# Layer 3's first chunk multiplied inside the last attention head

## The chip, the cores and the metric

The kernel runs on one core of a Trainium2 chip. Its time is the device time of one launch in microseconds (us). Before the change the median of three runs is 1751.03 us (1750.17 to 1754.02). TensorE (PE) does matrix products, VectorE (DVE), ScalarE (ACT) and GpSimd (POOL) do elementwise work, and SyncE (SP) issues most DMAs. PEld is TensorE's weight loading.

## The reference

Four graph layers follow each other on a graph of 2708 nodes with 512 features; each takes the layer-normed, relu'd features and adds its result to them. What matters here is the end of layer 2, attention with 8 heads, and the start of layer 3:

```python
# layer 2, per head h
e = where(adj > 0, leaky_relu(f1[:, None] + f2[None, :], 0.2), -9e15)
out = elu(softmax(e) @ Wh)
x = x + concat_heads(out)
# layer 3
h = maximum(layernorm(x), 0)
agg = (adj > 0) @ h / deg
x = x + relu(concat(h @ W_self + b_self, agg @ W_nb + b_nb) @ W_comb + b_comb)
```

The kernel has the weights of layer 3 multiplied together beforehand, so that layer 3 is one product of h with each of two fused matrices (`wfs` for the node itself, `wfn` for the neighbours), one bias row (`b3`), and an aggregation over the adjacency of the neighbour product.

## The kernel before

**Chunks.** The 2708 rows are cut into 22 chunks of 128 rows (`NC`; the last has 20). The functions with a chunk number `c` below handle one such chunk.

**Attention.** Ten units run one after the other: heads 0 and 7 in two halves of the target columns each, heads 1 to 6 whole. A unit has 22 steps, one per source chunk, so there are 220 steps; unit 9, the second half of head 7, has steps 198 to 219. In a step `s` the loop at L1443 to L1467 first prepares step `s + 3`: `scale` (ACT, tile `whs`, L1051 and L1053) and `make` (DVE, the attention weights, tile `t`, L1067). Then `multiply` (PE, L1297) adds step `s` into PSUM tiles `av` and `sums`. There are four buffers of `t` (`TILES`). After its last step a unit's sums are copied out by ACT (`evict`, L1337) and stored on SP's queue to `avT` and `sumT` (L1339).

**Order of the work.** The instructions are traced in program order, and a planner then orders those of each engine by its own costs, in favour of what stands first in the program. [...] A table `plan`, filled by `behind(step, function, chunk)`, says behind which step of the attention loop a piece of other work is written. The entries for layer 3 are counted back from the end of the attention: `(9, turn3, 0)` means step 220 - 9 = 211.

**From attention to layer 3, for one chunk.** `load3` (SP: `aT` from `avT` L1237, `sT` from `sumT` L1240, and the residual rows `x`); `turn3` (PE: a small product and four transpositions, L1246 and L1250; DVE: `rs` L1252 to L1255 and `y` L1257); `elu3` (POOL: `z = min(y, 0)` L1264; DVE: `x += max(y, 0)` L1265; ACT: Tanh and Exp of `z`, L1267 and L1268; DVE: L1269 and L1270, which use Exp(z) - 1 = (Exp(z) + 1) Tanh(z/2)); `save3` (a store of `x` on ACT's queue); `normalize3` (DVE L219, L221, ACT Sqrt L223, DVE L224, L234, tile `hn`); `transpose3` (PE L245, ACT L247, tile `hT`); `nb3` (PE: eight matmuls with `wfn`, L187; `halves` splits the result in two on ACT L298 and DVE L299); `self3` (PE: eight matmuls with `wfs`, L187; DVE adds `b3`, L1495; the store to `s3` is on ACT's queue). After these comes the aggregation (L424).

**Where they stand.** `nb3` and `self3` and the pool for their results (`ring3`) exist only after the attention: the loop over all 22 chunks at L1510 runs `nb3(c)`, `transpose3(c+1)`, `turn3(c+3)`, `normalize3(c+2)`, `save3(c+2)`, `elu3(c+3)`, `load3(c+5)`, `self3(c)`. Ahead of it, the attention's last steps do `turn3` of chunks 0 to 2, and `elu3`, `normalize3` and `transpose3` of chunk 0. `elu3`'s Tanh has a tile `th3` of its own with one buffer. Tiles tagged `t` (three buffers) hold `hn`, the `y` of `self3` and the copies of `evict`.

Of the kernel before, what the change touches and what calls it, by code (L numbers as in the profile page):

```python
# [44 lines left out]
def fast_layers(  # L45
# [46 lines left out]
    def rows(c):  # L92
        return min(R, N - c * R)

    def move(engine, dst, src):

        if dst.shape[0] == last_rows:
            cut = last_rows // 16 * 16
            engine.dma_start(dst[:cut], src[:cut])
            return engine.dma_start(dst[cut:], src[cut:])  # L100
        return engine.dma_start(dst, src)
# [106 lines left out]
    def any_product(c, po, lhsT, w, n):  # L208
        if c == NC - 1:
            product_of_last(po, lhsT, w)  # L210
        else:
            product(po, lhsT, w, n)
# [1008 lines left out]
    tails_w = tails.tile([P, len(middle), O + S], F32, name="tails_w")  # L1221
    nc.gpsimd.memset(tails_w, 0.0)
    tails_f = tails.tile([P, 3], F32, name="tails_f")
    kept3, l3_weights = {}, []


    def load3(c):
# [32 lines left out]
    def elu3(c):  # L1260

        xc, y = kept3[c]
        z = e3.tile([R, D], F32, name="z3")
        nc.gpsimd.tensor_scalar(z, y, 0.0, None, op0=ALU.min)  # L1264
        nc.vector.scalar_tensor_tensor(xc[:R], y, 0.0, xc[:R], op0=ALU.max, op1=ALU.add)  # L1265
        th = e3.tile([R, D], F32, name="th3", bufs=1)
        nc.scalar.activation(th, z, AF.Tanh, scale=0.5)  # L1267
        nc.scalar.activation(z, z, AF.Exp)  # L1268
        nc.vector.scalar_tensor_tensor(z, z, 1.0, th, op0=ALU.add, op1=ALU.mult)  # L1269
        nc.vector.tensor_tensor(xc[:R], xc[:R], z, ALU.add)  # L1270
        kept3[c] = xc

    def save3(c):
        n = rows(c)
        move(nc.scalar, x3[c * R : c * R + n, :], kept3[c][0][:n])

    def normalize3(c):
        kept3[c] = kept3[c], norm(kept3[c], R)
# [147 lines left out]
        behind(first + 2, count_neighbors, i)  # L1426

    for at_step, fn, c in (
        (16, load3, 0),
        (15, load3, 1),  # L1430
        (9, turn3, 0),
        (8, load3, 2),
        (8, elu3, 0),
        (6, normalize3, 0),
        (6, save3, 0),
        (6, turn3, 1),
        (5, load3, 3),
        (2, transpose3, 0),
        (2, turn3, 2),
        (1, load3, 4),  # L1440
    ):
        behind(len(steps) - at_step, fn, c)

    for s in range(len(steps)):
        if s == (len(units) - 3) * NC + 1:
            tails_ctx.close()
            e3_ctx = ctx.enter_context(ExitStack())
            e3 = e3_ctx.enter_context(
                tc.tile_pool(name="e3", bufs=2, side="right", reuse_waits="tile")
            )  # L1450
        if s + 6 < len(steps) and (s + 6) % NC % GROUP == 0:
            load_wh(s + 6)
        if s + 3 < len(steps):
            scale(s + 3)
            make(s + 3)
        if s + 1 < len(steps):
            compare(s + 1)
        multiply(s)
        multiply_sides(s - 1)
        for fn, args in plan.pop(s, ()):  # L1460
            if fn in (load_l3_weights, spread_nodes, split):
                with tc.issue_after(made[s]):
                    fn(*args)
            elif fn is mask:
                with tc.issue_after(scaled[s + 2]), tc.issue_after(made[s]):
                    fn(*args)
            else:  # L1467
                fn(*args)
# [4 lines left out]
    with ExitStack() as stack:  # L1473
        margin = stack.enter_context(tc.tile_pool(name="margin", bufs=1))
        margin.tile([P, 112], F32, name="margin")
        ring = stack.enter_context(tc.tile_pool(name="ring3", bufs=NC - 1, reuse_waits="tile"))
        b3 = ring.tile([P, D], F32, name="b3", bufs=1)
        nc.sync.dma_start(
            b3, bass.AP(tensor=bias3.tensor, offset=bias3.offset, ap=[[0, P], [1, D]])
        )  # L1480
        h3 = {}
        wself, wnb = l3_weights

        def nb3(c):
            pn = ps.tile([P, D], F32, name="nb3_ps", tag="ps")
            any_product(c, pn, kept3[c][1], wnb, R)
            h3[c] = halves(ring, pn, c)

        def self3(c):
            n = rows(c)  # L1490
            po = ps.tile([P, D], F32, name="self_ps", tag="ps")
            any_product(c, po, kept3.pop(c)[1], wself, R)
            y = common.tile([P, D], F32, name="y", tag="t", bufs=3)
            for own in corners if c == NC - 1 else [(slice(0, n), slice(0, D))]:
                ins = nc.vector.tensor_tensor(y[own], po[own], b3[own], ALU.add)  # L1495
                move(nc.scalar, s3[c * R : c * R + n, own[1]], y[own])
            return ins.ins

        def do(fn, c):
            if c < NC:  # L1500
                fn(c)


        elu3(1)
        normalize3(1)
        save3(1)
        elu3(2)
        for c in range(NC):
            nb3(c)
            if c:  # L1510
                do(transpose3, c + 1)
            do(turn3, c + 3)
            do(normalize3, c + 2)
            do(save3, c + 2)
            do(elu3, c + 3)
            do(load3, c + 5)
            final = self3(c)
            if c == 0:
                transpose3(1)

        e3_ctx.close()
        wk = stack.enter_context(
            tc.tile_pool(name="l3", bufs=2, side="right", reuse_waits="tile")
        )

        def weight3(m, cs):
            kt = wk.tile([R, WG], F32R, name="kt3", bufs=3)
            nc.vector.tensor_copy(by_chunk(kt, cs), pattern(m, cs))  # L1528
            return kt

        def judge():


            bad = const.tile([P, 7], F32, name="bad")

            nc.gpsimd.memset(squares[TAIL:, NC - 1], 0.0)
            nc.vector.tensor_reduce(
                bad[:, 0:1], squares.rearrange("p c g -> p (c g)"), AX.X, ALU.add
            )
            nc.vector.tensor_reduce(bad[:, 1:2], deg, AX.X, ALU.add)  # L1540
            nc.vector.tensor_tensor(bad[:, 0:1], bad[:, 0:1], bad[:, 1:2], ALU.subtract)
            nc.vector.tensor_reduce(bad[:, 2:3], deg, AX.X, ALU.min)
            nc.vector.tensor_scalar(bad[:, 2:3], bad[:, 2:3], 0.5, None, op0=ALU.is_lt)
            for i, (op, over, sign) in enumerate(((ALU.max, ALU.is_gt, 1), (ALU.min, ALU.is_lt, -1))):
                f = bad[:, 3 + i : 4 + i]
                nc.vector.tensor_reduce(f, f12.rearrange("p c h -> p (c h)"), AX.X, op)
                nc.vector.tensor_scalar(f, f, sign * F_MAX, None, op0=over)
                nc.vector.tensor_scalar(
                    bad[:, 5 + i : 6 + i], wmax[:, i : i + 1], sign * W_MAX, None, op0=over
                )  # L1550
            nc.vector.tensor_reduce(bad[:, 1:2], bad[:, 2:], AX.X, ALU.max)
            pv = ps.tile([P, 2], F32, name="verdict_ps", tag="ps")
            nc.tensor.matmul(pv[:1], ones, bad[:, 0:2], start=True, stop=True)

            differ = small.tile([1, 2], F32, name="differ")
            nc.vector.tensor_scalar(
                differ[:, 0:1], pv[:1, 0:1], float(N - P * NC), None, op0=ALU.not_equal
            )
            nc.vector.tensor_copy(differ[:, 1:2], pv[:1, 1:2])
            nc.vector.tensor_tensor(verdict, differ[:, 0:1], differ[:, 1:2], ALU.add)  # L1560

        def before3(c):
            if c == 2 * KMAX:
                with tc.issue_after(final):
                    judge()
            return load_x(x3, c), load_x(s3, c, name="sc", pool=wk, bufs=4)

        def after3(c, acc, loaded):
            n = rows(c)
            xc, sc = loaded  # L1570
            nc.vector.scalar_tensor_tensor(
                sc[:n], acc[:n], rdeg[:n, c : c + 1], sc[:n], op0=ALU.mult, op1=ALU.add
            )
            nc.vector.scalar_tensor_tensor(
                xc[:n], sc[:n], 0.0, xc[:n], op0=ALU.max, op1=ALU.add
            )
            half = max(1, n // 32) * 16 if c == NC - 1 else n
            nc.scalar.dma_start(out[c * R : c * R + half, :], xc[:half])
            if half < n:
                nc.sync.dma_start(out[c * R + half : c * R + n, :], xc[half:n])  # L1580

        aggregate(weight3, h3, before3, after3)
# [628 lines left out]
```

## Time and profile before

| | us |
|---|---|
| median of three runs | 1751.03 |
| the profiled execution, its own time | 1754.19 |
| its span, first to last instruction | 1752.3 |
| TensorE busy | 1724.1 (98%) |
| VectorE busy | 1312.2 (75%) |
| ScalarE busy | 845.6 (48%) |
| unit 9 begins on TensorE | 1309.95 |
| `nb3(0)` begins | 1354.90 |
| `nb3(1)` begins | 1368.13 |
| `nb3(2)` begins | 1376.15 |

All positions are us from the start of the span. In a timeline a row has start, length, engine, line, operation, `out<-in`, the engine's shape, and in square brackets how long the engine had been idle and what ended that. A matmul that waits in the pipeline still counts as busy, so PE's 98% is not 98% of its peak. The granted clock is TensorE's, 1.00 being full.

### The profile page before, as it was taken

The page shows a single profiled execution, that of the slowest core. Times are in us where ns is not written, and L with a number is a line of the kernel's source. Part 1 is how long each engine was busy: PE and PEld are TensorE (multiplying, and loading weights), DVE is VectorE, ACT ScalarE, POOL GpSimd, SP SyncE. Part 2 cuts the span into 40 slices and gives each one's busy share as a digit, 9 for nine tenths or more (in the row PEclk, how much of TensorE's full clock was granted, in tenths as well). Part 3 has the DMA queues.
Part 4 walks back from the last instruction along what each step waited for, and adds up shares of the span by engine and source line. Part 5 has one row for each costly group of instructions (what it writes and reads, how often), then busy time and mean ns, then how long its engine had stood idle before and what let it go on. Part 6 is the DMA issues. An engine that isn't in the chain of part 4 may idle for free.

```text
span 1752.3 us, 29486 instructions
## 1 busy us (share of the span) xinstructions
PE 1724.1 (98%) x11280; PEld 1078.8 (62%) x11280; DVE 1312.2 (75%) x1902; ACT 845.6 (48%) x1554; POOL 248.3 (14%) x252
## 2 busy tenths in 40 slices
PE   8999999999999999999999999999999999999998
PEld 5567777744468887644675665434434455588886
DVE  7759889855455556888899999999998677633334
ACT  5447777622210000366878888888794566400000
POOL 1003323311111112255000000000001222100000
PEclk9999999999999999999999999999999999999999
DMA  8436666444551111332420221022022444313221
GB/s 291 139 117 199 205 206 186 133 120 123 121 135 49 48 49 56 122 122 93 133 63 13 61 64 58 15 64 62 13 74 72 130 141 130 109 36 109 73 72 41
DMA packets 167227, 177.37 MB, mean 101 GB/s; under 512 B 84127, under 2 KB 106591, under 8 KB 166060
## 3 DMA queue, kind: packets, MB, share of 16 engines
q1 hardware_dynamic: 144428, 131.99, 27.2%
q10 hardware_dynamic: 18808, 33.37, 5.1%
q0 software_dynamic: 3840, 10.03, 1.5%
q8 instruction: 90, 1.47, 0.4%
q14 instruction: 61, 0.50, 0.1%
HBM read 111.64 MB, written 55.36 MB: 95 GB/s over the span
## 4 chain that ended last, share of the span: by engine, by line
PE 86%; DVE 8%; ACT 2%; issue 2%; DMA 1%; SPq 1%; POOL 0%; ACTq 0%; DVEq 0%; POOLq 0%
PE acc L424 36%; PE av L1297 17%; PE nb_ps L187 8%; DVE t L1067 5%; PE sums L1297 4%; PE h_ps L187 4%; PE line_ps L187 4%; PE self_ps L187 4%; PE hT_ps L245 2%; PE fused_ps L370 2%; PE wh_ps L187 1%; DVE wh_a L1114 1%; PE av_ps L1250 1%; ACT b L1085 1%; DVE f L1131 1%
## 5 line engine op out<-in xcount | busy, mean ns | idle before, releaser
L1067 DVE SCALAR_TENSOR_TENSOR t<-rb,ec,vT 128x2708 f32<-128x2708 f32 (+2 forms) x214 | 510.4, 2450 | 8.3 <-PE sums L1297 6.2
L1297 PE MATMUL av<-t,whs 128*32 128x451 f32 (+5 forms) x4432 | 445.5, 514 | 6.2 <-DVE t L1067 3.9
L424 PE MATMUL acc<-halves,kt 128*128 128x512 f32 x1848 | 426.5, 391 | 2.4 <-DVE kt L870 2.1
L424 PEld LDWEIGHTS acc<-halves,kt 128*128 128x128 f32 x1848 | 345.2, 188 | 79.7 <-DVE kt L870 6.6
L1085 ACT ACTIVATE b<-t,eb 128x2708 bf16<-128x2708 f32 (+1 forms) x119 | 285.0, 2395 | 33.3 <-DVE t L1067 33.2
L1297 PEld LDWEIGHTS av<-t,whs 128*32 128x32 f32 (+1 forms) x4432 | 193.2, 110 | 167.9 <-issue 118.5
L424 PE MATMUL acc<-halves,ar 128*128 128x512 f32 x924 | 243.6, 414 | 0.0
L424 PEld LDWEIGHTS acc<-halves,ar 128*128 128x128 f32 x924 | 172.6, 188 | 58.2 <-issue 20.6
L223 ACT ACTIVATE ln_rs<-ln_mv,eps 128x1 f32<-128x1 f32 x88 | 25.7, 295 | 306.3 <-DVE ln_mv L221 298.4
L870 DVE SCALAR_TENSOR_TENSOR kt<-lastr,index,vT 128x512 fp32r<-128x512 int16 (+3 forms) x154 | 112.5, 742 | 75.8 <-PE acc L424 75.4
L1528 DVE CAST kt<-vT 128x512 fp32r<-128x512 uint8 (+3 forms) x154 | 56.5, 368 | 131.3 <-PE acc L424 131.2
L1264 POOL TENSOR_SCALAR z<-y 128x512 f32<-128x512 f32 x22 | 44.1, 2005 | 639.5 <-DMA aT<-avT 513.6
L555 DVE TENSOR_TENSOR_SCAN cum<-ai,deg 128x512 int16<-128x512 int32 (+2 forms) x110 | 128.3, 1170 | 0.0
L598 ACT ACTIVATE cum<-cum,limit 128x512 int16<-128x512 int16 (+3 forms) x132 | 88.0, 667 | 51.6 <-DVE deg L563 49.4
L1297 PE MATMUL sums<-t,whs 128*32 128x325 f32 (+4 forms) x952 | 104.4, 451 | 0.0
L1051 ACT ACTIVATE whs<-wh,ef 128x64 f32<-128x64 f32 x214 | 72.5, 342 | 59.6 <-PE sums L1297 21.1
L219 DVE BATCH_NORM_STATS2 ln_st<-x 128x6 f32<-128x512 f32 x88 | 60.3, 687 | 48.3 <-DMA x<-x 34.1
L187 PE MATMUL nb_ps<-wfn,hT 128*128 128x512 f32 x168 | 78.7, 612 | 2.1 <-ACT hT L247 2.1
L187 PE MATMUL wh_ps<-w2s,hT 128*128 128x512 f32 x168 | 76.1, 595 | 1.0 <-ACT hT L247 0.9
L187 PE MATMUL h_ps<-w0s,hT 128*128 128x512 f32 x168 | 76.5, 598 | 0.0
L1297 PE MATMUL sums<-b,parts 128*32 128x338 bf16 (+2 forms) x884 | 76.0, 308 | 0.0
L549 ACT ACTIVATE ar<-ai 128x512 fp32r<-128x512 int32 (+2 forms) x132 | 75.0, 568 | 1.7 <-DMA ai<-in_adj 1.3
(211 smaller groups left out, 1952.7 us busy)
## 6 DMA issues: line engine op xcount, KB each, us to landing
x<-x SPq DMA_DIRECT2D x105, 256.0 KB
ai<-in_adj SPq DMA_DIRECT2D x84, 256.0 KB
x<-x ACTq DMA_DIRECT2D x84, 256.0 KB
x<-in_x SPq DMA_DIRECT2D x42, 256.0 KB
rb<-rT SPq DMA_DIRECT2D x7, 1354.0 KB
wh<-whd SPq DMA_DIRECT2D x63, 96.0 KB
packed<-two POOLq DMA_DIRECT2D x44, 128.0 KB, 3.3
whd<-wh SPq DMA_DIRECT2D x21, 256.0 KB
```

The costliest lines, as they stand in the source:

```text
L187: nc.tensor.matmul(po[:n], lhsT[:, f, :n], w[:, f, :], start=(f == 0), stop=(f == NF - 1))
L219: nc.vector.bn_stats(st[:n], xc[:n])
L424: nc.tensor.matmul(acc[:R], weight[:, k * R : (k + 1) * R], parts[:, i, :], start=(m == 0 and i == 0), stop=(m == NC - 1),)
L549: nc.scalar.activation(ar[:, :gw], ai[:, :gw], AF.Square, accum_out=squares[:R, m, g : g + 1])
L555: nc.vector.tensor_tensor_scan(cum[:n, :gw], ai[:n, :gw], ai[:n, :gw], 0.0 if g == 0 else deg[:n, m : m + 1], op0=ALU.add, op1=ALU.max,)
L598: nc.scalar.activation(cum[:n, :gw], cum[:n, :gw], AF.Sign, bias=limit[:n], scale=-1.0, accum_out=signs[:n, m, g : g + 1],)
L870: nc.vector.scalar_tensor_tensor(by_chunk(kt, cs), lastr[:, cs[0] * R : (cs[-1] + 1) * R].rearrange("p (c r) -> p c r", r=R), index[:R, m ...
L1051: ins = nc.scalar.activation(t[:q, :O], wh.pop((u, m))[:q], AF.Copy, scale=by)
L1067: ins = nc.vector.scalar_tensor_tensor(t[:q, : hi - lo], row[h][:q, lo:hi], ec[:q, m, h : h + 1], vT[g][:q, k, lo:hi], op0=ALU.max, op1=AL ...
L1085: nc.scalar.activation(b[:q, : hi - lo], weight[s][:, : hi - lo], AF.Sigmoid, bias=eb[:q, m, h : h + 1], scale=STEEP,)
L1297: nc.tensor.matmul(p[j * S : (j + 1) * S, : b - a], lhsT, rhs[:, part * size + a : part * size + b], start=(s % NC == 0), stop=(s % NC == ...
L1528: nc.vector.tensor_copy(by_chunk(kt, cs), pattern(m, cs))
```

## The change

Four things are edited.

1. The plan's entries for layer 3 are moved ahead and there are more of them: `turn3` and `elu3` of chunk 0 go from steps 211 and 212 to step 204, its `normalize3` and `save3` from 214 to 208, its `transpose3` from 218 to 212. Chunk 1's `elu3` and `normalize3`, which stood after the attention, go to steps 210 and 213, its `turn3` from 214 to 209, its `transpose3`, which stood behind the loop's first `self3`, to 218. `nb3(0)` and `self3(0)` stand behind steps 214 and 215. `turn3` of chunks 2 and 3 stands behind 216 and 219, `elu3` of chunks 2 and 3 behind 217 and 219, `normalize3(2)` behind 219.
2. `nb3` and `self3` become functions that exist ahead of the attention loop. A pool `first3` for chunk 0's split product and for `b3` is opened behind unit 7's first step, and `b3` is loaded there; `ring3` has one buffer fewer.
3. The loop after the attention starts at chunk 1.
4. Tanh writes over `y`, its source's source, instead of into `th3`, and L1269 reads it there.

```diff
-    kept3, l3_weights = {}, []
+    kept3, h3, l3_weights = {}, {}, []
...
-        th = e3.tile([R, D], F32, name="th3", bufs=1)
-        nc.scalar.activation(th, z, AF.Tanh, scale=0.5)
+        nc.scalar.activation(y, z, AF.Tanh, scale=0.5)
         nc.scalar.activation(z, z, AF.Exp)
-        nc.vector.scalar_tensor_tensor(z, z, 1.0, th, op0=ALU.add, op1=ALU.mult)
+        nc.vector.scalar_tensor_tensor(z, z, 1.0, y, op0=ALU.add, op1=ALU.mult)
...
+    def nb3(c):
+        pn = ps.tile([P, D], F32, name="nb3_ps", tag="ps")
+        any_product(c, pn, kept3[c][1], l3_weights[1], R)
+        h3[c] = halves(rings3[min(c, 1)], pn, c)
+
+    def self3(c):
+        n = rows(c)
+        po = ps.tile([P, D], F32, name="self_ps", tag="ps")
+        any_product(c, po, kept3.pop(c)[1], l3_weights[0], R)
...
-        (16, load3, 0),
-        (15, load3, 1),
-        (9, turn3, 0),
-        (8, load3, 2),
-        (8, elu3, 0),
-        (6, normalize3, 0),
-        (6, save3, 0),
-        (6, turn3, 1),
-        (5, load3, 3),
-        (2, transpose3, 0),
-        (2, turn3, 2),
-        (1, load3, 4),
+        (20, load3, 0),
+        (19, load3, 1),
+        (16, turn3, 0),
+        (16, elu3, 0),
+        (15, load3, 2),
+        (12, normalize3, 0),
+        (12, save3, 0),
+        (11, turn3, 1),
+        (10, load3, 3),
+        (10, elu3, 1),
+        (8, transpose3, 0),
+        (7, normalize3, 1),
+        (7, save3, 1),
+        (6, nb3, 0),
+        (5, self3, 0),
+        (4, turn3, 2),
+        (3, load3, 4),
+        (3, elu3, 2),
+        (2, transpose3, 1),
+        (1, turn3, 3),
+        (1, normalize3, 2),
+        (1, save3, 2),
+        (1, elu3, 3),
+        (1, load3, 5),
...
             tails_ctx.close()
+            first3 = ctx.enter_context(
+                tc.tile_pool(name="first3", bufs=1, side="right", reuse_waits="tile")
+            )
+            rings3 = [first3]
+            b3 = first3.tile([P, D], F32, name="b3")
+            nc.sync.dma_start(
+                b3, bass.AP(tensor=bias3.tensor, offset=bias3.offset, ap=[[0, P], [1, D]])
+            )
...
-        ring = stack.enter_context(tc.tile_pool(name="ring3", bufs=NC - 1, reuse_waits="tile"))
+        ring = stack.enter_context(tc.tile_pool(name="ring3", bufs=NC - 2, reuse_waits="tile"))
+        rings3.append(ring)
...
-        elu3(1)
-        normalize3(1)
-        save3(1)
-        elu3(2)
-        for c in range(NC):
+        for c in range(1, NC):
             nb3(c)
-            if c:
-                do(transpose3, c + 1)
+            do(transpose3, c + 1)
...
             final = self3(c)
-            if c == 0:
-                transpose3(1)
```

## The prediction

> **What bounds the kernel now.** I read the chain that ended last first: 86% of it is TensorE, so time is won only where TensorE idles or runs slow. A table of stretches then shows where that is (columns: busy us of PE, weight loads, DVE, ACT, POOL, with counts; granted clock; DMA share; GB/s):
>
> ```profile
> 1310.00:1320.00 10.00, 10.00 (x153) 4.89 (x155) 10.00 (x7) 5.08 (x17) 0.00 (x0) 1.00 0.42 99
> 1340.00:1354.00 14.00, 10.98 (x126) 5.23 (x130) 10.98 (x22) 8.47 (x17) 3.55 (x2) 0.88 0.30 83
> 1354.00:1373.00 19.00, 16.90 (x53) 7.98 (x46) 11.74 (x28) 10.05 (x17) 2.60 (x3) 0.82 0.44 133
> 1373.00:1400.00 27.00, 27.00 (x87) 13.55 (x86) 20.67 (x48) 16.86 (x22) 7.41 (x4) 1.00 0.44 133
> ```
>
> PE is full before 1340 and after 1373. Between lies the seam from the last attention unit to layer 3, with idle time and a low clock. TensorE's timeline shows both:
>
> ```profile
> 1346.24 1.30 PE L1297 MATMUL av<-t,whs 128*32 128x325 f32 x16 [1.19 <-DVE ln_mv L221]
> 1349.92 0.63 PE L245 MATMUL hT_ps<-ident,hn 128*128 128x128 f32 x4 [1.83 <-DVE hn L234]
> ...
> 1354.90 6.64 PE L187 MATMUL nb_ps<-wfn,hT 128*128 128x512 f32 x8
> 1361.38 0.29 PE L1246 MATMUL sums_ps<-mix,sT 80*128 80x16 f32 x2
> 1361.52 0.63 PE L1250 MATMUL av_ps<-ident,aT 128*128 128x128 f32 x4
> 1361.99 3.60 PE L187 MATMUL self_ps<-wfs,hT 128*128 128x512 f32 x8
> 1365.43 0.60 PE L245 MATMUL hT_ps<-ident,hn 128*128 128x128 f32 x4
> 1368.13 3.70 PE L187 MATMUL nb_ps<-wfn,hT 128*128 128x512 f32 x8 [2.10 <-ACT hT L247]
> ```
>
> Three waits, 1.19 + 1.83 + 2.10 = 5.1 us. And chunk 0's nb product takes 6.64 us where chunk 1's takes 3.70: the clock was halved from 1350.8 to 1360.9 (second windows at both ends):
>
> ```profile
> 1351.00:1352.00 1.00, 1.00 (x7) 0.36 (x9) 0.79 (x4) 1.00 (x3) 0.00 (x0) 0.50 0.85 261
> 1361.00:1362.00 1.00, 1.00 (x9) 0.76 (x8) 0.29 (x4) 0.42 (x1) 0.00 (x0) 1.00 0.05 16
> ```
>
> Why PE waits stands in DVE's timeline:
>
> ```profile
> 1336.54 1.56 DVE L1067 SCALAR_TENSOR_TENSOR t<-rb,ec,vT 128x1300 f32<-128x1300 f32 x1
> 1338.02 1.10 DVE L1265 SCALAR_TENSOR_TENSOR x<-y,x 128x512 f32<-128x512 f32 x1
> 1339.04 1.56 DVE L1067 SCALAR_TENSOR_TENSOR t<-rb,ec,vT 128x1300 f32<-128x1300 f32 x1
> 1342.40 0.69 DVE L1269 SCALAR_TENSOR_TENSOR z<-z,th 128x512 f32<-128x512 f32 x1 [1.80 <-issue]
> ```
>
> L1269 stands at the head of DVE 1.80 us until ACT's Exp is done; the weights (L1067) of the next steps queue behind it.
>
> **What the skill says.** "TensorE: Matmul & The Clock Gate", Part 1: the clock is half unless a free-running window of about 3.4 us was busy. The trace agrees: 1350.8 to 1360.9 is three such windows; at 820 to 828, after 2.66 us of waiting, it was one. The same page, in its architectural detail, calls ACT and DVE strictly first-in first-out; the 1.80 us above agrees. "ScalarE: Activation LUTs", What ACT_TABLE_LOAD costs: 1283 ns each; the trace has 1.28. "SBUF — State Buffer", SBUF: two separate sides: GpSimd and two-input DVE work exclude each other; here L1265 takes 1.10 beside POOL's z, 0.69 without.
>
> **The change, part by part.** Let t be us from 1309.95, the start of unit 9 (steps 198 to 219). Durations: a step on PE 1.64 (1313.41 to 1329.82 is ten), its weights on DVE 1.48; turn3 0.8 on PE (1333.23 to 1334.04); transposition 0.45; nb3 or self3 3.44.
>
> *TensorE's work up to nb3(1) is the same before and after*: 22 x 1.64 + 4 turn3 x 0.8 + 2 x 0.45 + nb3(0) + self3(0) 6.9 = 47.1. Before, nb3(1) starts at t = 58.2: 11.1 lost, of which 5.1 waits, 3.1 cold in nb3(0), 1.8 in the last step (1351.49 to 1354.90 against 1.64), 0.4 in turn3(2), the rest small gaps. So 11.1 is the most that can be won here.
>
> *DVE's work is what moves.* To the last weights DVE now has 22 x 1.48 = 32.6, two chunks of turn3 1.5 (1335.04 to 1336.54), elu 2.2 and norm 1.7 (0.73 + 0.2 + 0.17 + 0.6), and halves and bias add 0.7 each: 32.6 + 10.8 + 1.4 = 44.8. TensorE has 44.7 by then. DVE has no reserve: it enters unit 9 with none (PE waited 0.45 for t just before), gains 0.16 a step, and had three tiles of lead only by step 211, where turn3(0) stood before; now it comes at step 204.
>
> *Walk of the queues.* PE: turn3(0) t = 11.5 to 12.3. DVE finishes the weights of 207 at 13.3, turn3's rs and y by 14.9, 208 by 16.4, L1265 by 17.4, 209 by 18.9, and then waits for z as before: POOL 2.67, Tanh 0.63, a table load 1.28 and Exp 0.63 end at 20.6. L1269 and L1270 to 22.1, 210 at 23.6. PE was done with step 209 and turn3(1) at 21.3: idle 2.35. DVE: 211 at 25.1, statistics, 212 at 27.8, y(1), hn(0) at 29.4, 213 at 30.9, 214 at 33.1. PE waits 0.9 for 212 and 1.0 for 213, 0.5 for 214 (transposition(0) fits at 29.5). Then DVE is ahead: nb3(0) 34.8, self3(0) 39.9, turn3(2) ends 45.6, nb3(1) starts at t = 51.7. That is 58.2 - 51.7 = 6.5 earlier, with 4.7 of new waits. L1269 and the weights are the things late; the two matmul blocks of 3.44 are what let DVE catch up.
>
> *A cold window after the 2.35 wait* costs 1.7 (half of 3.4), and the 2.4 of waits behind it, which are DVE's, absorb most: 0 to 1.7 more, I take 0.4.
>
> *Chunk 2 has less time.* Between the end of turn3(2) and the transposition of chunk 2, PE had turn3(2) at 1351.5 and the transposition at 1371.7, 20 us. Now: steps 217 to 219 4.9, transposition 0.45, turn3(3) 0.8, nb3(1) 3.44 = 9.6. From y to the end of hn a chunk took 13.8, 15.3, 13.3, 8.1 and 10.1 us (chunks 0 to 4; 1373.84 to 1383.93 for the last). y(2) starts 1.1 after turn3(2), at 46.7, hn(2) is wanted at 55.1: waits of 0, 1.6 or 4.9 for 8.1, 10.1, 13.3. I take 1.6: makes of t are over by then, as for chunk 4.
>
> *Edits costed at nothing.* Tanh over y: it must now wait for L1265, which ends (17.4) before POOL's z (17.7); without that cover, the difference. y's slot is held to L1269, two chunks ahead of its reuse. b3's load leaves the seam (SP at 1358.25) for unit 7's second step, in SP's queue ahead of wh loads, where it waits for the last reader of tails_row, one matmul step; wh is loaded six steps ahead; uncovered, one step. load3(4) and load3(5) (aT, sT on SP) read columns that unit 8 has already written; the aT load of chunk 0 was issued at 1315.75, t = 5.8, before turn3(0) at 11.5. self3(0)'s store waits on ACT's queue for the bias add, inside a 3.44 block; save3 likewise holds ACT's whs, which is three steps ahead. Each: 0 to 1.6, taken 0. Table loads stay in number.
>
> *Sum*: 6.5 - 0.4 - 1.6 = 4.5 off; the profiled span 1752.3 becomes 1747.8 (its own time 1754.19 becomes 1749.7), and the median of the runs, 3.2 below that execution, 1751.03 - 4.5 = 1746.5. The loop after nb3(2) is PE-bound at 7.92 a chunk (1376.15 to 1384.07), so all of it arrives.
>
> **Rivals.**
> *Cold windows on the path.* If the mid-unit wait chills nb3(0) too, and the wait before chunk 2's transposition chills what follows, each adds 1.7: 4.5 - 3.4 = 1.1, 1749.9. For: 1.83 and 2.66 us waits were followed by half clock. Against: 2.10 at 1366.0 was not.
>
> *Chunk 2 comes late, slower.* Place: PE before the transposition of chunk 2. hn(2) takes the 13.3 that it took before, PE idles 4.9, and the clock stays low for three windows as before, 10.1 us at half: 5.1 lost. 6.5 - 4.9 - 5.1 = -3.5: 1754.5, and with the mid-unit chill 1756. It decides once wait and cold together exceed 6.5. For: ACT holds three output copies, hT(1), chunk 2's Tanh, Exp, Sqrt with their loads in one queue there. Against: 8.1 and 10.1 in the loop.
>
> *DVE never runs dry*, L1269 being queued behind more weights: the waits of unit 9 vanish with chunk 2 in time: up to 8.5 off, 1742.5. Against: the 1.80 of before.
>
> **How the numbers follow.** 0.2% (3.5 us) is about what a measurement tells from none. Main case 0.45, its own range 1744 to 1748.5; cold windows 0.28; chunk 2 late 0.23; DVE never dry 0.04. Nearly all of the main case (0.42) and the last lie below 1747.5: faster 0.46; the cold case and main's rest, with a little of the late one: same 0.32; slower 0.22. Range 1743.5 to 1755: it leaves out the far ends.
>
> **What would show it.** Right: nb3(1) some 6 us earlier relative to unit 9's start; PE waits of about 2 us for t near step 210; DVE idle ahead of L1269(0) about 1.8; all five nb3/self3 blocks at 3.4 to 3.7. Wrong: a block of nb or self near 6.6; a wait over 3 us before a transposition; ACT holding whs back; the loop's period above 7.92.

## The result, and the profile after

| | before | after |
|---|---|---|
| median of six runs, us | 1750.84 (1748.98 to 1754.02) | 1760.05 (1758.92 to 1761.56) |
| the profiled execution, its own time | 1754.19 | 1760.06 |
| its span | 1752.3 | 1758.3 |
| unit 9 begins on TensorE | 1309.95 | 1308.84 |
| `nb3(1)` begins | 1368.13 | 1361.94 |
| `nb3(2)` begins | 1376.15 | 1369.87 |
| `nb3(21)`, the last chunk, begins | 1525.49 | 1531.45 |

The ratio after to before is 1.0048 (95% interval 1.0038 to 1.0058): 9.2 us slower by the medians, 5.9 by the two profiled executions. The forecast was 1746.5.

**The seam became faster, as forecast.** The table of stretches of after (same columns as in the prediction) no longer has a thin stretch between 1340 and 1373; PE's busy time in its two rows was 10.98 of 14 and 16.90 of 19:

```profile
1340.00:1354.00 14.00, 14.00 (x100) 5.47 (x96) 11.09 (x14) 5.95 (x12) 1.42 (x1) 0.92 0.13 41
1354.00:1373.00 19.00, 19.00 (x134) 9.30 (x126) 11.88 (x29) 11.28 (x17) 6.30 (x4) 1.00 0.42 124
```

That is not the whole seam: what PE still waits for now lies just ahead of these rows. Up to `nb3(2)`, TensorE's timeline of after shows one wait where there were three, with one cold step (2.38 for an `av` group of 1.30) behind it; every nb and self block is at 3.6 or 3.7:

```profile
1338.14 0.63 PE L245 MATMUL hT_ps<-ident,hn 128*128 128x128 f32 x4 [2.42 <-DVE hn L234]
1338.70 2.38 PE L1311 MATMUL av<-t,whs 128*32 128x325 f32 x16
...
1343.81 3.70 PE L187 MATMUL nb_ps<-wfn,hT 128*128 128x512 f32 x8
...
1349.22 3.70 PE L187 MATMUL self_ps<-wfs,hT 128*128 128x512 f32 x8
...
1361.94 3.60 PE L187 MATMUL nb_ps<-wfn,hT 128*128 128x512 f32 x8
...
1369.87 3.60 PE L187 MATMUL nb_ps<-wfn,hT 128*128 128x512 f32 x8
```

Counted from the start of unit 9, `nb3(2)` begins at t = 61.03; before it was 66.20. That is 5.17 us won.

**The loop behind it lost more.** From `nb3(2)` to `nb3(21)` before takes 1525.49 - 1376.15 = 149.34 us, after 1531.45 - 1369.87 = 161.58. That is 12.24 lost. With unit 9 starting 1.11 earlier, -1.11 - 5.17 + 12.24 = +5.96, and the last `acc` block before the end indeed begins 5.97 later (1743.39 against 1737.42). A chunk takes 8.64 us in most of the loop, against 7.92.

The chain of waits of after between 1401 and 1500 (total us, times, longest) names it:

```profile
ACT y L1266 <- POOL z L1264: 41.9, 12, 3.5
DVE ln_rs L224 <- ACT ln_rs L223: 27.9, 11, 2.5
PE hT_ps L245 <- DVE hn L234: 5.8, 11, 0.5
```

In the same stretch of before neither DVE's wait for the Sqrt nor PE's for `hn` is there, and ACT waits for POOL less than half as long:

```profile
ACT th L1267 <- POOL z L1264: 16.7, 13, 1.4
```

ScalarE's timeline shows what is different. Before, one chunk of the loop (start, length, then the instruction):

```profile
1412.56 1.28 ACT L223 ACT_TABLE_LOAD   x1
1413.86 0.29 ACT L223 ACTIVATE ln_rs<-ln_mv,eps 128x1 f32<-128x1 f32 x1
1414.17 1.28 ACT L1267 ACT_TABLE_LOAD   x1
1416.70 0.63 ACT L1267 ACTIVATE th<-z 128x512 f32<-128x512 f32 x1 [1.25 <-POOL z L1264]
```

And after:

```profile
1421.96 0.63 ACT L1266 ACTIVATE y<-z 128x512 f32<-128x512 f32 x1 [3.48 <-POOL z L1264]
1422.60 1.28 ACT L223 ACT_TABLE_LOAD   x1
1423.90 0.29 ACT L223 ACTIVATE ln_rs<-ln_mv,eps 128x1 f32<-128x1 f32 x1
1424.21 1.28 ACT L1267 ACT_TABLE_LOAD   x1
```

The two table loads a chunk are still two. But the Sqrt of chunk c+2 now stands behind the Tanh of chunk c+3, and that Tanh waits 3.48 us for GpSimd. On VectorE the order turned as well. Before, a chunk's last elu sum (L1270) comes ahead of the next chunk's `turn3` work (L1252 to L1257):

```profile
1410.54 0.69 DVE L1270 TENSOR_TENSOR x<-x,z 128x512 f32<-128x512 f32 x1
1412.03 0.16 DVE L1252 TENSOR_TENSOR rs<-er,sums_ps 128x8 f32<-128x8 f32 x1 [0.80 <-PE sums_ps L1246]
...
1415.43 0.64 DVE L234 TENSOR_SCALAR hn<-x,ln_mv,ln_rs 128x512 f32<-128x512 f32 x1
```

After, the sum (L1269 now) stands behind the four short instructions of `turn3`, of which only `y` (L1257, at 1419.68) still follows it, and the reciprocal (L224) waits for the Sqrt:

```profile
1417.28 0.16 DVE L1252 TENSOR_TENSOR rs<-er,sums_ps 128x8 f32<-128x8 f32 x1 [0.34 <-PE sums_ps L1246]
...
1418.47 0.69 DVE L1269 TENSOR_TENSOR x<-x,z 128x512 f32<-128x512 f32 x1
...
1424.23 0.16 DVE L224 RECIPROCAL ln_rs<-ln_rs 128x1 f32<-128x1 f32 x1 [2.54 <-ACT ln_rs L223]
1424.42 0.55 DVE L234 TENSOR_SCALAR hn<-x,ln_mv,ln_rs 128x512 f32<-128x512 f32 x1
```

So `hn`, which before was done at 1416.07 for a transposition at 1419.18, 3.1 us in hand, is done at 1424.97 for one at 1425.12.

With nothing in hand the loop becomes a closed chain: each chunk's work starts only when the last chunk's has come round. From one transposition of after to the next: 0.80 on PE up to the first VectorE instruction of `turn3` (1416.48 to 1417.28), 3.08 on VectorE up to `y`, 1.56 to the end of POOL's `z`, 0.67 Tanh, 1.29 table load, 0.31 Sqrt, 0.20 reciprocal, 0.58 `hn`, 0.15 to PE: 8.64. The chain that ended last, followed back, reaches into the loop's last passes; its earliest pieces (start, us, what) are a part of this chain:

```profile
1515.47 1.49 POOL z L1264
...
1516.99 0.63 ACT y L1266
...
1518.93 0.30 ACT ln_rs L223
...
1519.46 0.56 DVE hn L234
...
1520.15 0.63 PE hT_ps L245 x4
```

Before, in the loop (1376 to 1530), this view was TensorE throughout.

### The profile page after: what moved, and what is told of

The parts are those of the page before. It is cut to its first block, busy times and chain, and to the rows that moved or that the text cites. A ratio compares the mean times of both kernels' runs of the same rounds, so it can differ in the third digit from the quotient of the medians.

```text
span 1758.3 us, 29478 instructions
## 1 busy us (share of the span) xinstructions
PE 1724.8 (98%) x11280; PEld 1074.2 (61%) x11280; DVE 1305.8 (74%) x1902; ACT 845.3 (48%) x1556; POOL 241.4 (14%) x252
## 5 line engine op out<-in xcount | busy, mean ns | idle before, releaser
L1264 POOL TENSOR_SCALAR z<-y 128x512 f32<-128x512 f32 x22 | 37.0, 1684 | 648.5 <-DVE y L1257 640.9
L598 ACT ACTIVATE cum<-cum,limit 128x512 int16<-128x512 int16 (+3 forms) x132 | 88.0, 667 | 51.7 <-DVE deg L563 49.5
L187 PE MATMUL self_ps<-wfs,hT 128*128 128x512 f32 x168 | 75.7, 593 | 0.0
```

What stands on the lines that cost most here:

```text
L187: nc.tensor.matmul(po[:n], lhsT[:, f, :n], w[:, f, :], start=(f == 0), stop=(f == NF - 1))
L598: nc.scalar.activation(cum[:n, :gw], cum[:n, :gw], AF.Sign, bias=limit[:n], scale=-1.0, accum_out=signs[:n, m, g : g + 1],)
```

## The experiments

The theory: the loop's order alone costs the 12 us, the seam's gain is real. Ratios are to runs of before made beside the others (medians 1751.72, 1751.88 and 1752.01 in the three groups). In the diffs, the lines that collect instructions into the lists `roots`, `tanhs` and `sums3` are left out, and comments are added; `issue_after` holds an instruction's place in its queue behind that of another.

### The Sqrt put back ahead of the Tanh

```diff
-            do(elu3, c + 3)
+            with tc.issue_after(roots[-1]):      # roots: the Sqrt of each norm
+                do(elu3, c + 3)
```

> The changed kernel with one constraint in the last loop: on ScalarE the Tanh of chunk c+3 is queued behind the Sqrt of chunk c+2, as it stood in the kernel before. Nothing else is altered. Order theory (the loss comes from the Sqrt standing behind a Tanh that waits for GpSimd's minimum): the loop's period falls from 8.64 to 7.92 us, TensorE's waits for hn vanish from it, and the 6.3 us that nb3(2) is earlier reach the end: 1750.8 - 6.3 = 1744.5 us (1743.5 to 1746). Rival (the period is longer because of where the tiles lie, of VectorE and GpSimd in each other's way, or of the number of table loads, none of which this touches): period stays 8.6, time stays at 1759 to 1761. Rival (the seam gained nothing that the end can use): 1750 to 1752.

Measured 1751.91 us, ratio 1.0002 (0.9994 to 1.0010). Neither the 1744.5 of the order theory nor the 1759 to 1761 of its first rival. The number is the second rival's (a seam that gained nothing, 1750 to 1752), but the traces are against that one: `nb3(2)` begins at t = 61.03 as in after. The loop from `nb3(2)` to `nb3(21)` takes 153.76 us, 8.17 a chunk, so 7.8 of the 12.2 us came back, and the 4.4 that did not come back ate most of the seam's gain. VectorE's timeline shows why not all:

```profile
1414.09 0.18 DVE L221 BATCH_NORM_AGGREGATE ln_mv<-ln_st 128x2 f32<-128x6 f32 x1
1415.34 0.16 DVE L224 RECIPROCAL ln_rs<-ln_rs 128x1 f32<-128x1 f32 x1 [1.06 <-ACT ln_rs L223]
```

`hn` follows at 1415.54 to 1416.09 and the transposition at 1416.14: still nothing in hand. On VectorE `turn3(c+3)` (from 1408.79) is still ahead of the elu sum of chunk c+2 (L1268 and L1269, 1411.03 to 1413.32) and its statistics. The theory was half of it: the order on VectorE counts too.

### The order of after forced on the kernel before

The text ahead of the loop is left as it is.

```diff
-            do(normalize3, c + 2)
-            do(save3, c + 2)
             do(elu3, c + 3)
+            with tc.issue_after(tanhs[-1]):      # the Tanh just traced
+                do(normalize3, c + 2)
+            do(save3, c + 2)
```

> The kernel before, its seam untouched, with the loop's order turned the other way: elu3(c+3) traced ahead of normalize3(c+2), and the Sqrt of c+2 queued behind the Tanh of c+3. Order theory: most chunks show Tanh, Sqrt, Exp on ScalarE, VectorE's reciprocal waits about 2.5 us for the Sqrt, TensorE waits about 0.5 us for hn in these chunks, and some 13 to 19 chunks x 0.72 us = 9 to 14 us are lost: 1760 to 1765 us. Rival (the order does no harm by itself; the loss belongs to the seam or to where tiles lie): within 2 us of 1750.8.

Measured 1780.58 us, ratio 1.0163 (1.0149 to 1.0177): 28.9 us slower, twice the size expected, in the expected direction and by the waits expected, though longer. Between 1401 and 1500 its Tanh waits longer than in after (4.78 us in one pass), VectorE waits up to 3.6 for the Sqrt, and PE up to 2.0 for `hn`:

```profile
1414.32 0.63 PE L245 MATMUL hT_ps<-ident,hn 128*128 128x128 f32 x4 [1.83 <-DVE hn L234]
```

From `nb3(2)` to `nb3(21)` it takes 1552.69 - 1380.26 = 172.43 us, 23.1 more than before; most of the rest is lost in passes 0 and 1, which in this kernel are in the loop too. Order alone, with the loop's work unaltered, costs this much. It is not quite the order of after: from 1420 on, in one pass of three, the Sqrt falls behind the Exp as well. Why it costs about twice what it does there is not shown.

### Tanh over `y` alone

```diff
-        th = e3.tile([R, D], F32, name="th3", bufs=1)
-        nc.scalar.activation(th, z, AF.Tanh, scale=0.5)
+        nc.scalar.activation(y, z, AF.Tanh, scale=0.5)
```

> The kernel before with one line of the change alone: Tanh writes over y, the tile th3 is gone. Order theory: ScalarE's queue in the loop still reads Sqrt, Tanh, Exp, so the period stays 7.92 and the time is that of before, 1750 to 1752 us. Rival (Tanh over y is the cause, since it must wait for VectorE's read of y and frees y later): a period of 8.3 to 8.7 and 1757 to 1766 us.

Measured 1751.25 us, ratio 1.0000 (0.9992 to 1.0008), and the loop at 149.34. This edit costs nothing and does not turn the order. The reverse, after with `th3` restored, was not run; but after_sum_first, below, has Tanh over `y` and a loop at 7.92.

### Products of chunk 0 one step later

```diff
-        (8, transpose3, 0),
+        (7, transpose3, 0),
-        (6, nb3, 0),
-        (5, self3, 0),
+        (5, nb3, 0),
+        (4, self3, 0),
```

> The changed kernel with the loop's constraint of after_sqrt_first, and in the seam transpose3(0), nb3(0) and self3(0) one step later (7, 5, 4 steps from the end in place of 8, 6, 5). In the changed kernel TensorE waits 2.42 us for hn(0) there and then runs one step at half clock (about 0.5 us). If that wait is simply hn being late, a step of 1.9 us takes up most of it: 2 to 2.5 us less than after_sqrt_first, about 1742 us. Rival (the wait turns up again at the next thing, hn(1) or the halves of nb3(0), or ScalarE's reshuffled queue delays the last weights): within 1 us of after_sqrt_first, or slower.

Measured 1751.51 us, ratio 1.0000 (0.9991 to 1.0008), against 1.0002 for after_sqrt_first: within 1 us, the rival's case. The wait of 2.42 us for `hn(0)` shrank to 0.36, but PE then waits 1.44 for `hT(0)`.

### A second profile of before

No edit.

> The kernel before, unaltered, profiled once more. Its first profile belongs to an execution of 1754.19 us, 2.5 us above the median of its runs. Theory (the 11.1 us lost in its seam were read from an unlucky execution, since whether the clock stays low there for three windows differs from one execution to the next): a profiled execution of about 1750 to 1752 us shows chunk 0's nb product at about 3.7 us in place of 6.64, and nb3(2) 2 to 4 us earlier relative to unit 9's start than the 66.2 of the first. Rival (the low clock is part of the kernel, and the times differ for another reason): 6.6 us again, and t = 66 within 0.5, whatever the execution's time.

Measured: a median of 1750.92 us and a ratio of 0.9995 (0.9986 to 1.0004), which is what no change reads as; the profiled execution took 1752.34. PE's nb products of chunks 0 and 1 there:

```profile
1353.74 3.70 PE L187 MATMUL nb_ps<-wfn,hT 128*128 128x512 f32 x8
...
1365.11 5.27 PE L187 MATMUL nb_ps<-wfn,hT 128*128 128x512 f32 x8 [3.18 <-ACT hT L247]
```

The three half-clock windows of the first profile are absent, chunk 0's product takes 3.70 in place of 6.64, and `nb3(2)` begins at t = 1374.70 - 1310.83 = 63.87 in place of 66.20. (The 5.27 is chunk 1's: after the longer wait, 3.18 in place of 2.10, the clock was 0.50 from 1365 to 1368.) The loop takes the same 149.35. So 2.3 us of the seam's loss belonged to that one execution. The profile of before_tanh_y agrees: 3.70 for chunk 0's product, and `nb3(2)` at t = 62.71.

### VectorE's order put back

```diff
-            do(turn3, c + 3)
+            with tc.issue_after(sums3[-1]):      # sums3: the last sum of each elu3
+                do(turn3, c + 3)
```

> The changed kernel with one other constraint in the loop: on VectorE the elementwise work of turn3(c+3) is queued behind the last sum of elu3(c+2), as it stood in the kernel before; ScalarE's Sqrt then comes ahead of the next Tanh by itself. Phase theory (the loop loses because each chunk's elu and norm run a phase later than before, so that hn is ready only as TensorE asks for it; mending ScalarE's order alone left 8.17 us): hn is ready 1.5 to 3 us ahead of its transposition, the period is 7.92, and the time is about 18 x 0.25 = 4.5 us below after_sqrt_first, 1747 to 1748 us. Rival (the 0.25 us come from something else, such as GpSimd's minimum beside VectorE's product at 1.10 us): the period stays 8.17 and the time at 1751 to 1752.

Measured 1746.61 us, ratio 0.9970 (0.9960 to 0.9981): 5.3 us faster than before. The phase theory expected 1747 to 1748; its period and its time in hand came. ScalarE has Sqrt, Tanh, Exp again without being told. VectorE's `hn` is done at 1416.39 and the transposition begins at 1418.69:

```profile
1415.75 0.64 DVE L234 TENSOR_SCALAR hn<-x,ln_mv,ln_rs 128x512 f32<-128x512 f32 x1
```

The loop takes 1517.08 - 1367.73 = 149.35 us, 7.92 a chunk. Between after (1.0048) and this kernel (0.9970) one line of order makes 13.7 us. 12.2 of it is the loop. GpSimd's minimum is longer in this order, as in before (1.99 us, 1.48 in after), so its length is not what made after slow.

### The same with the products moved

after_sum_first with the edit of after_sqrt_tr0; then with nb and self yet one step later, at `(4, nb3, 0)` and `(3, self3, 0)`.

> after_sum_first with chunk 0's transposition, nb and self product one step later (7, 5, 4 steps from the end). In after_sqrt_tr0 this placing had nb3(2) 1.6 us earlier relative to turn3(0) than in the changed kernel, and no cold window. If the loop is bound by TensorE at 7.92 now, these 1.6 us arrive: about 1746 us. Rival (the loop is still bound by VectorE and ScalarE, and what TensorE gains at the seam is waited for again): the same as after_sum_first within 0.5 us.

> after_sum_tr0 with chunk 0's nb and self product one more step later (4 and 3 steps from the end), transposition as there. In after_sqrt_tr0 TensorE waited 1.44 us for hT(0) ahead of nb3(0). If that wait is simply hT late, one step takes it up: 1 to 1.4 us less than after_sum_tr0, about 1745 us. Rival (the product later lets the halves and the bias add of chunk 0 fall on chunk 1's and 2's norm, and the wait comes back there): equal to after_sum_tr0 or slower.

Measured 1746.06 us, ratio 0.9969 (0.9958 to 0.9979), and 1745.29 us, ratio 0.9960 (0.9946 to 0.9974). Both are faster than before, the second has the lowest time of all the kernels; the intervals do not part the three from each other. `nb3(2)` begins at t = 59.34 in after_sum_first, 59.40 and 58.09 in these two. So the first move gained nothing at the seam: its 1746 came out by luck, since after_sum_first lay lower than expected. The 1.6 us expected of it were a misreading: the profile of after that they were read against had a cold window, which after_sum_first does not show. The second move has the 1 to 1.4 us expected of it in the trace (1.31), but its time alone could not tell.

### One constraint in one pass

```diff
+            if c == 1:
+                with tc.issue_after(roots[-1]):
+                    do(elu3, c + 3)
+            else:
                 do(elu3, c + 3)
```

> The changed kernel with one constraint in one chunk: in the loop's first pass (c = 1) alone, Tanh of chunk 4 is queued behind the Sqrt of chunk 3; the other 20 passes are left as the planner sets them. Entry theory (the planner's order of the loop is carried from chunk to chunk, and the seam's new plan only starts it the wrong way round): the later passes keep Sqrt, Tanh, Exp on ScalarE and the order of before on VectorE, the period is 7.92 from about the fifth pass on, and the time is that of after_sum_first or up to 2 us more (a pass or two of transition), 1746.5 to 1749 us. Rival (the order falls back, or the period is long for a reason that isn't the order): 8.2 to 8.6 us a chunk, 1752 to 1760 us.

Measured 1750.42 us, ratio 0.9995 (0.9986 to 1.0003), above the 1746.5 to 1749 expected. On the order the entry theory (the order is carried from pass to pass) held: from `nb3(4)` (1390.15) to `nb3(19)` (1508.95) every one of the 15 passes takes 7.92 us, with no further constraint. The one pass of transition, from `nb3(3)` at 1377.91 to `nb3(4)`, was undervalued: 12.24 us, with a wait of 2.51 for `hn` and a low clock behind it, 4.3 lost. That the loop's start decides is shown. Which of the other edits (an entry of the seam's plan, the pools, or the loop's start at chunk 1) starts it the wrong way round stays open.

### GpSimd's minimum doubled

```diff
         nc.gpsimd.tensor_scalar(z, y, 0.0, None, op0=ALU.min)
+        if c > 3:
+            nc.gpsimd.tensor_scalar(z, y, 0.0, None, op0=ALU.min)
```

Once in after, once in after_sum_first; the same values are computed twice.

> The changed kernel with GpSimd's minimum of chunks 4 and up computed twice, one after the other, into the same z: 1.48 us more work a chunk on an engine that is idle most of the time. Closed-chain theory (in the changed kernel's loop, transposition, turn3, y, GpSimd's z, Tanh, table load, Sqrt, hn and the next transposition follow each other without slack): the period grows by all of it, from 8.64 to about 10.1 us, some 15 chunks x 1.5 = 22 us: about 1782 us. Rival (the period is set by the amount of work on VectorE or ScalarE, or by transfers): 1760 to 1764 us.

> The same doubled minimum of chunks 4 and up in after_sum_first, where hn is ready 2.3 us ahead of its transposition. Closed-chain theory: the 1.5 to 2 us more are taken from that slack and TensorE doesn't wait: 1746.5 to 1749 us. Rival (doubled work on GpSimd costs whatever the order is, by keeping VectorE from the memory): as much as in after_z2, 20 us or more.

Measured 1788.55 us, ratio 1.0212 (1.0195 to 1.0229), and 1762.77 us, ratio 1.0065 (1.0048 to 1.0082). In after the period grew from 8.64 to 10.21 (from one nb product to the next, 1431.00 to 1441.21), that is by the whole 1.57 us of a second minimum with its gap; PE's transposition, which waited 0.53 us for `hn` in after, waits 2.10:

```profile
1426.49 0.63 PE L245 MATMUL hT_ps<-ident,hn 128*128 128x128 f32 x4 [2.10 <-DVE hn L234]
```

The closed chain is shown by that. (The time is 6 us above the 1782 expected: the passes from `nb3(2)` and `nb3(4)` took 11.84 and 11.99.) In after_sum_first the expectation failed: 16.2 us more, not 0 to 2.4. Passes of 8.44 and 8.92 us took turns, and PE waited up to 0.8 for `hn`. The slack had been read from `hn` alone, 2.3 us. There is a second chain, the elu's own, closed through VectorE's queue: in after_sum_first `y` ends at 1414.91, minimum, Tanh and Exp follow, the product (L1268) begins at 1418.34, 3.43 later, and from a product's start to the end of the next chunk's `y` it is 4.49 (1410.42 to 1414.91). Together 7.92, the period itself, of which only a wait of 0.48 for `halves` is spare. 7.92 - 0.48 + 1.57 = 9.0, near the longer of the two passes. In the trace of the doubled kernel the chain closes: from the end of `y` to the product it takes 5.00 us in both kinds of pass, and from the product to the end of the next `y` 3.92 where `halves` stands behind the product and 3.45 where it stands ahead of it: 8.92 and 8.45. The product's wait for Exp there (the product is L1270 in this kernel; 1.4 at most in after_sum_first):

```profile
DVE z L1270 <- ACT z L1269: 32.0, 12, 2.9
```

The rival, that doubled work on GpSimd keeps VectorE from the memory, does not show: VectorE's product and its L1265 (L1267 here) take 0.692 us on average in both kernels. So the loop at 7.92 has two limits nearly level, TensorE and the elu's chain. The same doubling cost 16.2 us there and 28.5 in after.

### The two products at the end of the head

```diff
-        (6, nb3, 0),
-        (5, self3, 0),
...
+        (1, nb3, 0),
+        (1, self3, 0),
         (1, turn3, 3),
```

> after_sum_first with nb3(0) and self3(0) moved from 6 and 5 steps before the end of the last head to its last step, ahead of turn3(3): the elementwise work stays early, the two products no longer part the head's steps. Prediction's theory (the two blocks of 3.44 us are what lets VectorE catch up with the weights): TensorE waits 2 to 4 us for t or for hn in the last steps, with a cold window or two: 1748.5 to 1752 us. Rival (VectorE is ahead of TensorE anyway, and only the early elementwise work counts): within 1 us of after_sum_first, 1746 to 1747.5 us.

Measured 1748.66 us, ratio 0.9977 (0.9968 to 0.9985), 3.4 us faster than before against 5.3 for after_sum_first; the intervals overlap. `nb3(2)` begins at t = 60.40, 1.06 later. PE waits 1.04 for `hn(1)`, beside the 2.42 for `hn(0)` that after_sum_first has too, and not at all for `t`. The time is at the lower end of the range of the prediction's theory and above the rival's 1747.5, but the 2 to 4 us of waits that the theory asked for did not come. So most of the seam's gain is the early elementwise work, and about 1 us by the traces is due to parting the steps with the two products; the 1.9 by the medians is not clear of the noise.

## Why the prediction was wrong

**The step that failed** is the last of its sum: "The loop after nb3(2) is PE-bound at 7.92 a chunk (1376.15 to 1384.07), so all of it arrives." It was read from the profile of before, where it is true, and carried over to a kernel whose loop makes the same calls but has another order on ScalarE and VectorE. In its place the runs show a loop bound by a closed chain at 8.64, 12.2 us longer. With the order restored in one line (after_sum_first) the time is 1746.61 us against the forecast of 1746.5. The list of what would show it wrong names the loop's period above 7.92, but no rival gave it a chance or a price, and the range ended at 1755.

**The seam's steps**, against the profile of after:

- *TensorE's work up to `nb3(1)` is the same; it begins at t = 51.7.* It began at 53.1. Direction and size are right: 5.1 earlier than before, 6.5 forecast.
- *A wait of 2.35 for weights at step 210, L1269 at the head of VectorE for 1.8.* Wrong in place. VectorE's timeline of after shows two further tiles of weights queued ahead of that product (L1268 now), so VectorE does not stand idle for it:

```profile
1327.55 3.04 DVE L1067 SCALAR_TENSOR_TENSOR t<-rb,ec,vT 128x1300 f32<-128x1300 f32 x2
1330.61 0.69 DVE L1268 SCALAR_TENSOR_TENSOR z<-z,y 128x512 f32<-128x512 f32 x1
```

  `hn(0)` is later for it, and PE waited 2.42 there instead. The four waits for weights that were forecast (4.7 in all) became this one.
- *A cold window costs 0.4.* It cost 1.69 in the profiled execution of after: `nb3(0)` begins at t = 34.97, in after_sum_first, whose wait is the same 2.42 but whose clock stayed at 1.00, at 33.28. The estimate let later waits for weights absorb it, and there were none.
- *Chunk 2's transposition waits 1.6.* It did not wait: from the start of `y(2)` to the end of `hn(2)` it was 9.2 us (1355.97 to 1365.21), between the 8.1 and 10.1 named.
- *4.5 off at the seam.* 5.17 in the profiles, 5.3 in the medians of after_sum_first. That these agree with the forecast is partly luck: 5.1 in place of 6.5 at `nb3(1)` and no wait in place of 1.6 cancel, and 2.3 us of the loss before belonged to one execution. Against the second profile of before, after gained 63.87 - 61.03 = 2.84 and after_sum_first 4.53. With 2.84 the sum comes near the medians too: 12.24 - 2.84 = 9.4, and 9.2 was measured.
- *Tanh over `y` and the other edits at nothing; the table loads stay in number.* Right. before_tanh_y shows the first, the timelines show two loads a chunk. Their number was the wrong question: their place in the queue changed.
- *Two blocks of 3.44 let VectorE catch up.* Worth 1 to 2 us at most (after_sum_ends), with no wait for weights in either kernel.
- *L1265 takes 1.10 beside POOL's z, 0.69 without.* In the walk this came true (1.10 at 1326.53). But it is no rule: in before, at 1348.33, it takes 0.69 with z running from 1348.38, and in the loop of after 0.72 (1420.88) inside z's 1.48.

**The rivals.** All three were about the seam. Neither cold windows on the path (1749.9) nor chunk 2 late (1754.5) is what made it slower, though one cold window was there. The third (chance 0.04) had VectorE's order right: the elu's product stood behind more weights, and PE never waited for `t`. But the wait moved to `hn(0)`, so its 1742.5, whose 8.5 off was not worked out, was not reached either.

## What to carry to other kernels

When an edit ahead of a loop changes what state the loop is entered in, and a planner or a list scheduler sets the order of the queues, the loop's period of before is not a constant: ask which order keeps each engine's next wait short, price the other order as a rival (here two swaps were worth 12 us over 19 passes), and pin the good one with a constraint. Slack has to be followed round every closed chain of the loop, not read at one tile. And a seam's loss should be read from more than one execution before it is called what can be won.

## What was not expected of the hardware

The same wait had different outcomes. In after, after_sqrt_first, after_sqrt_c1, after_z2 and after_sum_z2 the wait of 2.42 us (2.43 in one) for `hn(0)` was followed by one stretch of half clock, and `nb3(0)` began at t = 34.97 or 34.98. In after_sum_first, whose seam is the same, it was not followed by one, and `nb3(0)` began at 33.28; after_sum_ends had the same wait and a clock of 1.00 from 1336 to 1348. The Trainium skill, "TensorE: Matmul & The Clock Gate", Part 1, says that the window in which activity is counted is free-running, so that the same kernel sees different numbers of cold matmuls; these traces, each one execution, agree with it, and give 1.69 us as the difference. So do the two profiles of before: the first had the low clock from 1350.8 to 1360.9, 10.1 us; in the second the clock was 1.00 from 1350 to 1362, and 0.50 from 1365 to 1368.
